# The values' stage of a latent attention: three pairs of banks for the scores, eight places for exponentials, one add in four on VectorE

## The chip, the cores and the metric

The kernel runs on one core of a Trainium2 chip. The metric is the device time of one execution in microseconds; the time of a version is the median of its runs. Everything is computed in float32, apart from some flags of a comparison in bfloat16.

## The reference

Two transformer layers over an input of 2 sequences of 1024 tokens, 512 wide, each with a layer norm ahead of each of its two halves and a residual add behind it. Layer 0 is a gated delta-rule attention and a feed-forward with 4-bit weights. Layer 1 is the attention that the change touches, and a gated feed-forward whose hidden units are kept two of four. Layer 1's attention, for one sequence (16 heads, keys and queries 16 wide, values 32 wide):

```python
q_latent = x @ wq_d                      # 512 -> 64
kv_latent = x @ wkv_d                    # 512 -> 64
q = rope(q_latent @ wq_u)                # 16 heads x 16
k = rope(kv_latent @ wk_u)
v = kv_latent @ wv_u                     # 16 heads x 32
attn = softmax(q @ k.T / sqrt(16))       # no mask: 1024 x 1024 a head
out = (attn @ v) @ wo                    # 512 -> 512
```

Layer 1's feed-forward is `sparsify_2to4(silu(x @ w_gate) * (x @ w_up)) @ w_down` with 2048 hidden units.

## The kernel before

The program is a Python script that is unrolled completely. Four engines (TensorE, VectorE, ScalarE, GpSimd) execute their instructions in exactly the order in which the script issues them. The loads and stores wait in one queue, SP's, and are issued from it one after the other; the planner chooses that order. Waits are derived from the tiles: a tile is taken from a pool with a fixed number of places for its tag (`bufs`), and an instruction that writes a new tile waits until the place that it was given is free.

PSUM has eight banks, which the class `Banks` hands out in three ways. `two` gives a pair of neighbouring banks (1024 columns), two such tiles at a time; `one` gives single banks, two at a time; `acc` holds one bank called `av` and one called `den`, and `side` gives these two in turn to smaller work. So four banks are `two`'s, two are `one`'s and two are `acc`'s.

`weave(main, fill)` sets the order of the work around the change. Both are generators. Each time `main` yields a number, that number is added to what is due, and steps of `fill` are issued until nothing is due. A step of the fill yields `STEP` = 3.4. What is left of the fill at the end of `main` is issued then.

Layer 1's attention of sequence 0 (the generator `first`, `att.run(0, ...)`) is woven with layer 0's feed-forward of sequence 1. In what the text calls the third part, the attention of sequence 1 (the generator `third`, `att.run(1, ...)`) is woven with layer 1's feed-forward of sequence 0 (`Sparse.run`). A step of that fill is four fp32 matmuls of 128x128 by 128x512. In the fourth part layer 1's feed-forward of sequence 1 runs alone (`Sevens`).

`Latent.run` makes the keys and values of a sequence, and then goes through two blocks of 512 queries, each in two stages. `scores` finds each query's largest score, which needs a reduction on VectorE (line 1515), and puts it as a 17th feature beside the 16 of the query, so that it is subtracted by the product itself. `values` is the stage that the change touches. It has 32 units, four groups of four heads by eight tiles of 128 keys. For each unit u:

- `weights(u)` (line 1559): four matmuls, one a head, in four groups of 32 rows of the array, write scores (keys by queries) into two tiles of `banks.two`; ScalarE takes the exponential of each tile (1024 wide, line 1574) into tiles `es`, of which there are six places.
- `gather(u - 1)`: four matmuls add the values' product into the bank `av` (line 1582). After the last unit of a group VectorE copies it to `oT`.
- In the third part (`running` false), for odd u, `pair(u)`: GpSimd adds the four heads' exponentials of unit u into those of unit u - 1, in place, 512 wide (line 1596). Then `total(u - 2)`: four matmuls with ones add the sums of an earlier pair into the bank `den` (line 1603).
- After a group's last total, four `divide` steps are put into the list `late`: VectorE takes the reciprocal of 128 columns of `den` and multiplies `oT` by it (lines 1634, 1635). Up to three of them are issued after each unit.
- The stage yields `per_value` after each unit. It is 3.0 for sequence 0 and 0.1 in the third part.

`project` multiplies `oT` by the output weights `wo`, adds the result to x and stores it. The steps of `output` for the first block are issued between the scores of the second block, and those for the second block at the end; there each of them is followed by a step of fill. In the third part the normalised result is also turned into `xT` for the fourth part (`follow`). With `keep_wo` (the third part) `wo` is loaded once, at the start; without it `output` loads it for each block.

Of the kernel before, what the change touches and what calls it, by code (L numbers as in the profile page):

```python
# [26 lines left out]
F32 = mybir.dt.float32  # L27
# [3 lines left out]
AF = mybir.ActivationFunctionType  # L31
# [5 lines left out]
P = 128  # L37
B, T, DM = 2, 1024, 512
NT = B * T // P
TT = T // P  # L40
KC = DM // P
# [11 lines left out]
NH1, HALF, DV = 16, 16, 32  # L53
LAT = 64
QB = 512
# [1306 lines left out]
class Latent:  # L1362
# [42 lines left out]
            nc.tensor.transpose(ps[:, gr * P : (gr + 1) * P], src[:, 4 * gr : 4 * gr + 4, :], self.core.ident)  # L1405
        nc.scalar.copy(dst, ps.rearrange("p (g t) -> p g t", g=4))

    def run(self, b, side, parked, out, per_score, per_value, keep_wo, running, beside=None, xT=None):

# [2 lines left out]
        core, nc, banks = self.core, self.core.nc, self.banks  # L1414
        p = core.pools(f"l_one{b}", side=side)
        self.tmp = core.pools(f"l_tmp{b}", 1, side=side)
        now = []

        def stage(name):
            if now:  # L1420
                core.pools.close(now.pop())
            if name:
                now.append(f"l_{name}{b}")
                return core.pools(now[0], 2, side=side)

        two = stage("k")
        beside = beside(lambda: two) if beside else iter(())
        for n in self.ns:
            nc.gpsimd.memset(n[:, :, HALF : HALF + 1], 1.0)
        wo = []  # L1430
        if keep_wo:
            wo.append(p.tile([P, KC, DM], F32, name="wo1"))
            nc.sync.dma_start(out=wo[0], in_=self.wo_in)
        lat = p.tile([P, T], F32, name="lat")
        kT = p.tile([P, 4, T], F32, name="kT1")
        v = p.tile([P, TT, NH1, DV], F32, name="v1")
# [116 lines left out]
        def values(q2, oT):  # L1553

            units = [(gr, kt) for gr in range(4) for kt in range(TT)]
            es, av, den, acc = {}, {}, {}, {}
            late = deque()

            def weights(u):
                gr, kt = units[u]  # L1560
                tiles = [banks.two("st_ps") for _ in range(2)]
                for h4 in range(4):
                    r = 32 * h4
                    nc.tensor.matmul(  # L1564
                        tiles[h4 // 2][:, h4 % 2 * 512 : h4 % 2 * 512 + 512],
                        kT[r : r + CR, gr, kt * P : (kt + 1) * P],
                        q2[r : r + CR, gr, :],
                        start=True,
                        stop=True,
                    )  # L1570
                es[u] = []
                for e in range(2):
                    t = two.tile([P, 2, QB], F32, tag="es", bufs=6, name="es")
                    nc.scalar.activation(t.rearrange("p i q -> p (i q)"), tiles[e], AF.Exp, scale=HALF**-0.5)  # L1574
                    es[u].append(t)

            def gather(u):
                gr, kt = units[u]
                if kt == 0:
                    av[gr] = banks.acc.tile([P, QB], F32, tag="av", name="av_ps")  # L1580
                for h4 in range(4):
                    nc.tensor.matmul(  # L1582
                        av[gr][32 * h4 : 32 * h4 + 32, :],
                        v[:, kt, 4 * gr + h4, :],
                        es[u][h4 // 2][:, h4 % 2, :],
                        start=(kt == 0),
                        stop=(kt == TT - 1),
                    )
                if kt == TT - 1:
                    nc.vector.tensor_copy(oT[:, gr, :], av.pop(gr))  # L1590

            def pair(u):

                for h4 in range(4):
                    t = es[u - 1][h4 // 2][:, h4 % 2, :]
                    nc.gpsimd.tensor_add(t, t, es[u][h4 // 2][:, h4 % 2, :])  # L1596

            def total(u):
                gr, kt = units[u]
                if kt == 1:  # L1600
                    den[gr] = banks.acc.tile([P, QB], F32, tag="den", name="den_ps")
                for h4 in range(4):
                    nc.tensor.matmul(  # L1603
                        den[gr][32 * h4 : 32 * h4 + 32, :],
                        self.ones,
                        es[u - 1][h4 // 2][:, h4 % 2, :],
                        start=(kt == 1),
                        stop=(kt == TT - 1),
                    )
                if kt == TT - 1:  # L1610
                    for q in range(QT):
                        late.append(lambda q=q, ps=den[gr]: divide(gr, q * P, ps))

            def add(u):

                gr, kt = units[u]
                if kt == 1:
                    acc[gr] = two.tile([P, 4, QB], F32, tag="acc", bufs=1, name="acc")
                for e in range(2) if kt else ():
                    t = acc[gr][:, 2 * e : 2 * e + 2, :]  # L1620
                    nc.vector.tensor_add(t, es[u - 1][e] if kt == 1 else t, es[u][e])  # L1621

            def total_run(gr):
                den = banks.acc.tile([P, QB], F32, tag="den", name="den_ps")
                for h4 in range(4):
                    nc.tensor.matmul(
                        den[32 * h4 : 32 * h4 + 32, :], self.ones, acc[gr][:, h4, :], start=True, stop=True
                    )
                for q in range(QT):
                    late.append(lambda q=q: divide(gr, q * P, den))  # L1630

            def divide(gr, q, ps):
                rd = two.tile([P, P], F32, tag="rd", name="rd")
                nc.vector.reciprocal(rd, ps[:, q : q + P])  # L1634
                nc.vector.tensor_mul(oT[:, gr, q : q + P], oT[:, gr, q : q + P], rd)

            for u in range(len(units) + 3):
                if u < len(units):
                    weights(u)
                if 0 <= u - 1 < len(units):  # L1640
                    gather(u - 1)
                if running:
                    if 0 <= u - 1 < len(units):
                        add(u - 1)
                    if u > TT and u % TT == 1:
                        total_run(u // TT - 1)
                elif u % 2:
                    if u < len(units):
                        pair(u)
                    if u >= 3:  # L1650
                        total(u - 2)
                yield per_value
                for _ in range(min(3, len(late))):
                    late.popleft()()
            for f in late:
                f()
# [23 lines left out]

        def output(qb, oT):

            if not keep_wo:
                wo[:] = [two.tile([P, KC, DM], F32, tag="wo", bufs=1, name="wo1")]
                nc.sync.dma_start(out=wo[0], in_=self.wo_in)
            turned[0] = fetch(b * TT + qb * QT)
            steps = [lambda: None] + [lambda t=t: project(qb, oT, t) for t in range(QT)]
            if xT is None:
                return steps

            def both(t):
                if t < QT:
                    project(qb, oT, t)
                follow(qb * QT + t)

            return steps[:1] + [lambda t=t: both(t) for t in range(QT + 3)]

        extra = []
        for qb in range(T // QB):
            two = stage("s")  # L1700
# [6 lines left out]
            two = stage("v")  # L1707
            oT = p.tile([P, 4, QB], F32, tag="oT", name="oT1")
            yield from values(q2, oT)
        two = stage("s")  # L1710
# [284 lines left out]
def two_layers(ctx, tc, a):  # L1995
    nc = tc.nc
    core = Core(ctx, tc)
    pools = core.pools
    banks = Banks(ctx, tc)
# [10 lines left out]
    parks = [[tc.dram_tile([P, DM], F32, name=f"park{i}_{n}") for n in range(NT)] for i in range(3)]  # L2010
# [10 lines left out]
    with tc.manual_schedule(engines={ENG.PE, ENG.DVE, ENG.Activation, ENG.Pool}):  # L2021
# [16 lines left out]
        att = Latent(core, banks, pools("l_w", side="right"), a)  # L2038


        def first():
            yield from att.run(0, "right", parks[0], parks[1], 3.4, 3.0, False, True, beside=factors.make)
            xs = pools("x2", side="right")
            core.hold(xs, 0)
            for n in range(TT):
                nc.sync.dma_start(out=core.x[n], in_=parks[1][n])
            yield 2 * STEP
            xT = pools("xT_2", side="right").tile([P, KC, T], F32, name="xT2")
            yield from norms(core, banks, core.x[:TT], xT)
            done.append(xT)  # L2050

        done = []
        factors = Factors(core, a)
# [6 lines left out]
        def third():  # L2060
            xT = pools("xT_3").tile([P, KC, T], F32, name="xT3")
            done.append(xT)
            yield from att.run(1, None, parks[0], parks[1], 3.4, 0.1, True, False, xT=xT)
            x = pools("x3").tile([P, TT, DM], F32, name="x_last")
            held.append(x)
            for n in range(TT, NT):
                core.x[n] = x[:, n - TT, :]
                nc.sync.dma_start(out=core.x[n], in_=parks[1][n])
# [77 lines left out]
```

## Time and profile before

| | |
|---|---|
| median of 3 runs | 3213.23 us (3211.96 to 3216.2) |
| profiled execution | 3214.91 us, span 3213.2 us |
| mean granted TensorE clock | 0.979 |
| busy: TensorE, VectorE, ScalarE, GpSimd | 97%, 60%, 29%, 24% |
| third part's stages of values | 2450 to 2555 us and 2754 to 2863 us |
| last matmul of the fill | 2899 us |
| first matmul of the fourth part | 2906.55 us |

All times inside the profile are microseconds from the start of the span. An instruction is named by its line, its engine and its tiles as "written <- read". A fp32 matmul is recorded as two passes, so that the four matmuls of a unit appear as eight records; neighbouring records of one kind are merged into one row with its start and its length. The row ends with the idle time of the engine before it, and what ended that, in square brackets. A TensorE row is busy while any of its matmuls is in flight, so a busy TensorE need not be one at its best pace. "PEld" is the load of weights into the array.

### The profile page before, as it was taken

To read this page: it belongs to the slowest core of one execution; us is meant where nothing else is said; L and a number is where in the kernel's file an instruction comes from. 1 tells how busy PE (TensorE), PEld (TensorE's weight loads), DVE (VectorE), ACT (ScalarE), POOL (GpSimd) and SP (SyncE) were. 2 spreads that over 40 slices of the span, in tenths; PEclk is the share of its full clock that TensorE was granted. 3 is DMA by queue.
4 is the path that set the end of the run, shared out by engine and by line. 5 is a ranking of instruction groups with operands and counts; after the bars stand their busy time and mean duration, and the time that the engine had idled before them with its cause. 6 is when DMAs were issued, how large, how long until landed. Compare 5 with 4: busy or idle time off the path is not lost.

```text
span 3213.2 us, 35654 instructions
## 1 busy us (share of the span) xinstructions
PE 3106.8 (97%) x13012; PEld 1626.1 (51%) x13012; DVE 1925.1 (60%) x3569; ACT 931.2 (29%) x1338; POOL 766.6 (24%) x822
## 2 busy tenths in 40 slices
PE   7999899999999999999999999999999999999998
PEld 6787754555555554555434444446433243224547
DVE  6888752466666554367577656745674367244766
ACT  5544311122222211311453125522113401432221
POOL 3323101122222211356321221222003600450000
PEclk9999899999999999999999999999999999999999
DMA  2111234132332224246112111142010010015211
GB/s 90 35 29 29 67 96 142 32 122 91 97 95 86 76 94 164 70 137 207 66 37 69 53 48 37 35 141 72 20 40 1 14 53 14 7 37 167 76 46 49
DMA packets 194638, 228.08 MB, mean 71 GB/s; under 512 B 53728, under 2 KB 148448, under 8 KB 194080
## 3 DMA queue, kind: packets, MB, share of 16 engines
q1 hardware_dynamic: 194464, 225.81, 22.2%
q8 instruction: 103, 1.69, 0.2%
q14 instruction: 71, 0.58, 0.1%
HBM read 153.11 MB, written 72.61 MB: 70 GB/s over the span
## 4 chain that ended last, share of the span: by engine, by line
PE 81%; DVE 9%; POOL 2%; issue 2%; ACT 2%; DMA 2%; SPq 1%; DVEq 0%; POOLq 0%; ACTq 0%
PE z_ps L1018 23%; PE o_ps L201 12%; PE z_ps L1064 8%; PE u_ps L201 5%; PE g_ps L201 5%; PE st_ps L1564 5%; PE s_ps L1506 4%; PE av_ps L1582 3%; PE proj_ps L201 2%; PE small_ps L630 1%; PE wide_ps L640 1%; DVE cv L469 1%; PE wide_ps L558 1%; DVE rd L1634 1%; PE den_ps L1603 1%
## 5 line engine op out<-in xcount | busy, mean ns | idle before, releaser
L991 ACT COPY part<-z_ps 128x512 f32<-128x512 f32 x288 | 168.7, 586 | 738.4 <-PE z_ps L1018 505.5
L1018 PE MATMUL z_ps<-xT,z_left 128*128 128x512 f32 x768 | 361.8, 601 | 3.1 <-DMA z_left<-in_w_gate 3.0
L1515 DVE TENSOR_REDUCE top<-s_ps 128x2 f32<-128x1024 f32 x256 | 301.0, 1217 | 80.4 <-PE s_ps L1506 80.3
L1574 ACT ACTIVATE es<-st_ps 128x1024 f32<-128x1024 f32 x256 | 248.3, 1021 | 175.9 <-PE st_ps L1564 171.0
L1018 PE MATMUL z_ps<-xt,z_left 128*128 128x512 f32 x576 | 274.3, 598 | 1.2 <-DVE z_h L1036 1.0
L1018 PEld LDWEIGHTS z_ps<-xT,z_left 128*128 128x128 f32 x768 | 142.0, 191 | 191.6 <-issue 164.0
L201 PE MATMUL o_ps<-w_down,h 128*128 128x512 f32 x512 | 229.6, 599 | 0.4 <-DVE part L1052 0.4
L1596 POOL TENSOR_TENSOR es<-es 128x512 f32<-128x512 f32 x128 | 159.3, 1276 | 148.7 <-ACT es L1574 78.0
L1018 PE MATMUL z_ps<-xT,w_left 128*128 128x512 f32 x384 | 181.5, 602 | 5.0 <-DVE part L1052 2.7
L1564 PE MATMUL st_ps<-q,kT 17*128 17x512 f32 x1024 | 178.3, 650 | 4.3 <-ACT es L1574 1.1
L1018 PEld LDWEIGHTS z_ps<-xt,z_left 128*128 128x128 f32 x576 | 106.2, 190 | 145.7 <-issue 123.3
L1052 DVE TENSOR_TENSOR part<-z_ps,part 128x512 f32<-128x512 f32 x108 | 74.4, 689 | 174.1 <-PE z_ps L1018 168.5
L1506 PE MATMUL s_ps<-kT,q 16*128 16x512 f32 x1024 | 156.6, 647 | 6.6 <-DVE top L1515 6.6
L201 PEld LDWEIGHTS o_ps<-w_down,h 128*128 128x128 f32 x512 | 95.2, 191 | 110.5 <-issue 106.3
L201 PE MATMUL proj_ps<-xT,wqkv 128*128 128x256 f32 x576 | 136.6, 392 | 12.2 <-ACT gw L427 12.2
L1582 PE MATMUL av_ps<-es,v 128*32 128x512 f32 x1024 | 138.9, 615 | 0.0
L1018 PE MATMUL z_ps<-xt,w_left 128*128 128x512 f32 x288 | 137.0, 598 | 0.7 <-DVE part L1052 0.7
L1053 POOL TENSOR_TENSOR h<-h,part 128x512 f32<-128x512 f32 x48 | 66.5, 1387 | 280.1 <-DVE part L1052 280.1
L1621 DVE TENSOR_TENSOR acc<-acc,es 128x1024 f32<-128x1024 f32 x96 | 131.7, 1419 | 0.0
L201 PEld LDWEIGHTS proj_ps<-xT,wqkv 128*128 128x128 f32 x576 | 109.3, 195 | 31.6 <-ACT gw L427 15.1
L1036 DVE TENSOR_TENSOR h<-z_ps,part 128x512 f32<-128x512 f32 x84 | 57.9, 690 | 102.4 <-PE z_ps L1018 89.3
L201 PE MATMUL o_ps<-sdown,h 128*128 128x512 f32 x256 | 117.1, 601 | 0.0
(311 smaller groups left out, 5164.9 us busy)
## 6 DMA issues: line engine op xcount, KB each, us to landing
sums<-factor SPq DMA_DIRECT2D x24, 512.0 KB, 3.3
kept_gate<-w_left SPq DMA_DIRECT2D x12, 896.0 KB, 3.7
kept_up<-w_left SPq DMA_DIRECT2D x12, 896.0 KB, 3.9
z_left<-kept_gate SPq DMA_DIRECT2D x12, 896.0 KB, 4.6
z_left<-kept_up SPq DMA_DIRECT2D x12, 896.0 KB, 4.6
kept_down<-w_down SPq DMA_DIRECT2D x16, 512.0 KB, 3.0
wd<-kept_down SPq DMA_DIRECT2D x16, 512.0 KB, 4.2
xl<-park SPq DMA_DIRECT2D x32, 256.0 KB, 2.7
```

Of the source, the lines that this page charges most:

```text
L201: nc.tensor.matmul(ps, lhsT, rhs, start=(i == 0), stop=(i == len(pairs) - 1))
L991: self.core.nc.scalar.copy(t, src)
L1018: self.core.nc.tensor.matmul(ps, left[l][:, k, :], self.right[r][:, k, :], start=(first and k == 0), stop=(k == 1), skip_group_check=True,)
L1052: nc.vector.tensor_add(v, ps, v)
L1064: nc.tensor.matmul(ps[:, i * dm : (i + 1) * dm], left[l][:, k, i * P : (i + 1) * P], right[r][k], start=(first and i == 0 and k == 0), sto ...
L1506: nc.tensor.matmul(tiles[h4 // 2][:, h4 % 2 * 512 : h4 % 2 * 512 + 512], q1s[t][r : r + HALF, gr, :], kT[r : r + HALF, gr, j * 512 : (j + ...
L1515: nc.vector.tensor_reduce(top[:, j, h : h + 2], tiles[e].rearrange("p (i k) -> p i k", i=2), AX.X, ALU.max, negate=True)
L1564: nc.tensor.matmul(tiles[h4 // 2][:, h4 % 2 * 512 : h4 % 2 * 512 + 512], kT[r : r + CR, gr, kt * P : (kt + 1) * P], q2[r : r + CR, gr, :], ...
L1574: nc.scalar.activation(t.rearrange("p i q -> p (i q)"), tiles[e], AF.Exp, scale=HALF**-0.5)
L1582: nc.tensor.matmul(av[gr][32 * h4 : 32 * h4 + 32, :], v[:, kt, 4 * gr + h4, :], es[u][h4 // 2][:, h4 % 2, :], start=(kt == 0), stop=(kt == ...
L1596: nc.gpsimd.tensor_add(t, t, es[u][h4 // 2][:, h4 % 2, :])
L1621: nc.vector.tensor_add(t, es[u - 1][e] if kt == 1 else t, es[u][e])
```

## The change

In the third part (`alone`, that is `per_value == 0`):

- the two tiles of scores of a unit come from `spot`, which gives a tile of `banks.two` twice and then two tiles of `banks.one`, in turn; a tile made of single banks gets two exponentials of 512 columns instead of one of 1024;
- `es` has eight places instead of six;
- the fourth of a pair's adds is issued on VectorE, the other three stay on GpSimd;
- after a group's last total, VectorE copies the bank `den` whole to a tile `dn` in SBUF, and the divisions read that, with the reciprocal in place;
- `per_value` is 0 instead of 0.1, so that no step of the fill is issued within the stage;
- `keep_wo` is gone: the output weights are loaded by `output`, for each of the two blocks.

For sequence 0 the stage keeps its two pairs, its six places and its order; there `es` is summed by `add`, which is not touched.

```diff
+        alone = per_value == 0
...
-        if keep_wo:
-            wo.append(p.tile([P, KC, DM], F32, name="wo1"))
-            nc.sync.dma_start(out=wo[0], in_=self.wo_in)
...
-                tiles = [banks.two("st_ps") for _ in range(2)]
+                tiles = [spot() for _ in range(2)]
...
-                        tiles[h4 // 2][:, h4 % 2 * 512 : h4 % 2 * 512 + 512],
+                        tiles[h4 // 2][h4 % 2],
...
-                for e in range(2):
-                    t = two.tile([P, 2, QB], F32, tag="es", bufs=6, name="es")
-                    nc.scalar.activation(t.rearrange("p i q -> p (i q)"), tiles[e], AF.Exp, scale=HALF**-0.5)
+                for tile in tiles:
+                    t = two.tile([P, 2, QB], F32, tag="es", bufs=8 if alone else 6, name="es")
+                    if len(tile) == 3:
+                        nc.scalar.activation(t.rearrange("p i q -> p (i q)"), tile[2], AF.Exp, scale=HALF**-0.5)
+                    else:
+                        for i in range(2):
+                            nc.scalar.activation(t[:, i, :], tile[i], AF.Exp, scale=HALF**-0.5)
                     es[u].append(t)
+
+            def spot():
+                count[0] += 1
+                if alone and count[0] % 3 == 0:
+                    return [banks.one("st_ps") for _ in range(2)]
+                tile = banks.two("st_ps")
+                return [tile[:, :QB], tile[:, QB:], tile]
...
-                    nc.gpsimd.tensor_add(t, t, es[u][h4 // 2][:, h4 % 2, :])
+                    eng = nc.vector if alone and h4 == 3 else nc.gpsimd
+                    eng.tensor_add(t, t, es[u][h4 // 2][:, h4 % 2, :])
...
                 if kt == TT - 1:
+                    dn = two.tile([P, QB], F32, tag="dn", bufs=1, name="dn")
+                    nc.vector.tensor_copy(dn, den.pop(gr))
                     for q in range(QT):
-                        late.append(lambda q=q, ps=den[gr]: divide(gr, q * P, ps))
+                        late.append(lambda q=q: divide(gr, q * P, dn, dn[:, q * P : (q + 1) * P]))
...
-            def divide(gr, q, ps):
-                rd = two.tile([P, P], F32, tag="rd", name="rd")
+            def divide(gr, q, ps, rd=None):
+                if rd is None:
+                    rd = two.tile([P, P], F32, tag="rd", name="rd")
                 nc.vector.reciprocal(rd, ps[:, q : q + P])
...
-            if not keep_wo:
-                wo[:] = [two.tile([P, KC, DM], F32, tag="wo", bufs=1, name="wo1")]
-                nc.sync.dma_start(out=wo[0], in_=self.wo_in)
+            wo[:] = [two.tile([P, KC, DM], F32, tag="wo", bufs=1, name="wo1")]
+            nc.sync.dma_start(out=wo[0], in_=self.wo_in)
...
-            yield from att.run(1, None, parks[0], parks[1], 3.4, 0.1, True, False, xT=xT)
+            yield from att.run(1, None, parks[0], parks[1], 3.4, 0, False, xT=xT)
```

## The prediction

> **What bounds the kernel now.** I read the views in this order: the page's groups, to find the lines that the change touches; the third part's busy time by stretches; the order of time, engine by engine, inside one stretch; and the granted clock around its ends.
>
> The two groups of the page that the change touches (columns: operation, count, busy us, mean ns of one, then idle time before and what ended it):
>
> ```profile
> L1574 ACT ACTIVATE es<-st_ps 128x1024 f32<-128x1024 f32 x256 | 248.3, 1021 | 175.9 <-PE st_ps L1564 171.0
> L1596 POOL TENSOR_TENSOR es<-es 128x512 f32<-128x512 f32 x128 | 159.3, 1276 | 148.7 <-ACT es L1574 78.0
> ```
>
> Only the third part uses POOL's adds (128 of them: two stages of values, sixteen pairs of units each, four heads). So that is where to look. In order of time, TensorE over one pair of units (start, length):
>
> ```profile
> 2459.10 1.07 PE L1582 MATMUL av_ps<-es,v 128*32 128x512 f32 x8
> 2460.10 1.32 PE L1564 MATMUL st_ps<-q,kT 17*128 17x512 f32 x8
> ...
> 2467.43 1.06 PE L1582 MATMUL av_ps<-es,v 128*32 128x512 f32 x8
> 2468.31 1.04 PE L1603 MATMUL den_ps<-es,ones 128*32 128x512 f32 x8
> 2469.28 1.14 PE L1564 MATMUL st_ps<-q,kT 17*128 17x512 f32 x8
> 2470.36 1.06 PE L1582 MATMUL av_ps<-es,v 128*32 128x512 f32 x8
> 2471.53 2.04 PE L1564 MATMUL st_ps<-q,kT 17*128 17x512 f32 x8
> 2473.51 1.06 PE L1582 MATMUL av_ps<-es,v 128*32 128x512 f32 x8
> 2474.39 1.04 PE L1603 MATMUL den_ps<-es,ones 128*32 128x512 f32 x8
> ...
> 2486.98 1.07 PE L1603 MATMUL den_ps<-es,ones 128*32 128x512 f32 x8 [0.26 <-DVE rd L1634]
> ```
>
> ScalarE and GpSimd over the same pair:
>
> ```profile
> 2470.46 1.94 ACT L1574 ACTIVATE es<-st_ps 128x1024 f32<-128x1024 f32 x2 [1.81 <-PE st_ps L1564]
> 2472.79 1.94 ACT L1574 ACTIVATE es<-st_ps 128x1024 f32<-128x1024 f32 x2 [0.39 <-PE st_ps L1564]
> ```
>
> ```profile
> 2468.62 4.95 POOL L1596 TENSOR_TENSOR es<-es 128x512 f32<-128x512 f32 x4 [1.13 <-PE av_ps L1582]
> 2474.70 4.96 POOL L1596 TENSOR_TENSOR es<-es 128x512 f32<-128x512 f32 x4 [1.13 <-PE av_ps L1582]
> ```
>
> A pair takes 6.08 us (2468.31 to 2474.39), and one chain fills it. Scores of the even unit start at 2469.28; their exponentials start 1.18 later; two of these take 1.94; only then is the second pair of banks free for the second half of the odd unit's scores. That is why the odd unit's scores take 2.04 and the even unit's 1.14: the four heads normally stream side by side, and here two run, then two more, 0.98 each. Behind them come the values' product (0.88 to the next start) and the denominator (0.97), and the next even unit. 1.18 + 1.94 + 0.15 + 0.98 + 0.88 + 0.97 = 6.10. So two pairs of banks pace the stage. GpSimd is idle 1.13 of each 6.08, ScalarE 2.2, and TensorE's 97% hides a split, not work. Once in a group of eight units the denominator also waits for its bank, which four reciprocals still read: 24.79 us a group (GpSimd's 2493.39 to 2518.18) against 4 x 6.08 = 24.32.
>
> The ends of the two stages, by stretches (busy us of PE, PEld, DVE, ACT, POOL; then the granted clock):
>
> ```profile
> 2562.71:2566.12 3.41, 0.71 (x2) 0.00 (x0) 3.31 (x7) 0.00 (x0) 0.00 (x0) 1.00 0.00 0
> 2566.12:2576.36 10.24, 9.03 (x15) 3.53 (x16) 6.98 (x12) 0.00 (x0) 0.00 (x0) 0.50 0.01 2
> 2753.86:2757.27 3.41, 2.30 (x14) 0.61 (x12) 2.54 (x6) 1.62 (x2) 0.00 (x0) 1.00 0.20 77
> 2757.27:2770.92 13.65, 13.65 (x56) 2.75 (x52) 0.00 (x0) 6.24 (x7) 6.18 (x6) 0.50 0.01 1
> 2772.00:2857.00 85.00, 82.60 (x552) 20.26 (x552) 21.54 (x27) 54.32 (x57) 67.51 (x56) 1.00 0.00 1
> ```
>
> TensorE went to half clock twice: behind the first stage, and at the second's start, which has no fill between its first two units and so leaves TensorE idle for 1.11 us there.
>
> **The change, part by part.**
>
> *Three pairs of banks.* Tiles of scores go round three pairs (the third made of two single banks), so a tile waits for the exponential of the tile three back. For an odd unit that is, for its first half, the second tile of the unit before the last (read long since), and, for its second, the first tile of the even unit. The chain loses one exponential: 1.18 + 1.02 + 0.15 + 0.98 + 0.88 + 0.97 = 5.18. The floor with no wait is 1.08 + 1.00 + 1.08 + 0.88 + 0.97 = 5.01 (starts in the lines above). I take 5.2 a pair. A tile in single banks takes two 512-wide exponentials; the nearest row, a 512-wide ScalarE copy, is 0.586 us, so 1.17 instead of 1.02. ScalarE then needs, for four tiles of which 4/3 are such, 4 x 1.02 + 1.33 x 0.15 = 4.28: under 5.2.
>
> *One add in four on VectorE.* GpSimd's chain falls from 4.95 to 3 x 1.24 = 3.71. VectorE's add is 0.69 (its 512-wide add from a bank; half of its 1.22 for 1024 from SBUF gives 0.61). If the two disturb each other: next to GpSimd the 128-wide product of the division took up to 1.41 against 0.29 alone, so up to 1.12 longer, and GpSimd's four adds took 5.06 instead of 4.95. Ends: 3.71 and 3.71 + 0.69 = 4.40, both under 5.2. Cover: the total is due two units later, some 5.2 + 1.95 after the scores began, and the adds are through at 2.2 + 4.4 = 6.6. Without this edit GpSimd's 4.95 plus its shortest restart (2462.55 - 2457.16 = 5.39) would pace the stage. VectorE's queue behind the add holds the divisions; it has four adds, two copies of 0.69 and 5.0 us of divisions in a group of 20.8.
>
> *Eight places for exponentials.* Four units in flight instead of three: nothing by itself, needed by the step above (an exponential of unit u+3 would otherwise wait for adds of unit u).
>
> *Sums copied out.* A copy of about 0.69 on VectorE frees the denominator's bank before the four divisions (4 x 1.24) instead of after; the 0.47 a group goes, three times a stage. The copy itself lies beside TensorE's next two units.
>
> *No fill in the stages.* With 0 instead of 0.1 per step, the fill steps at 2451.25, 2555.02 and 2858.46 (eight matmuls, 3.43 us each at full pace) run later, when TensorE has nothing else: I count them as work in both kernels, at no gain. Bounds for where they land: the last turn before the fourth part has TensorE waits of 0.89, 1.66 and 3.02, so up to 2.6 less, or nothing.
>
> *A stage, walked.* Scores 0 at 0; scores 1 start at 1.08 and their second half at 1.18 + 1.02 + 0.15 = 2.35, done at 3.33; the first values' product follows, scores 2 start at 4.4. Fifteen pairs at 5.2 bring 82.4. Then a product of 1.0 and the wait for GpSimd's last adds: last scores at 79.3, adds from 81.6, three of 1.24 plus 0.55 for the disturbance, last matmuls 0.55: end at 86.4. Before: first stage 2450.18 to 2555.02 = 104.84, less 3.43 of fill, 101.4; second 2754.48 to 2863.09 = 108.61, less 3.43, 105.2 (it has the half clock). Gains 15.0 and 18.8.
>
> *Behind the first stage.* The next scores wait for a reduction that stands in VectorE's queue behind the four divisions, and those stood behind the fill's add and comparisons. Before: 2555.02 to 2567.33, two fill steps in it, so 12.31 - 7.26 = 5.05 of loss. After: copy 0.9, divisions 5.0, first reduction 1.2, so 7.1 with one fill step of 3.6: 3.5. Gain 1.5. TensorE still idles 2.4 us there, so I leave the half clock (about 3.9 us of loss) as it is.
>
> *The output weights, loaded twice.* The 1 MB load leaves p, and with it its 8 KB per partition, and is issued at each output(), on SP ahead of the loads of x (SP already stood there 111.8 us for the end of the stage, so what is behind it starts no earlier). It takes 5.8 (4.3 to 7.4) from issue to landing. Behind the first stage the first projection comes some 9 us in: hidden. At the end, the projection waited until 2869.45, 6.36 after the last sum, for reciprocals that held its bank; with the copy that wait is gone, and the load, landing at 0.3 + 5.8 = 6.1, takes its place: 0; ends -2.7 (its place is free early) and +1.4.
>
> Sum: 15.0 + 18.8 + 1.5 + 0 = 35.3. The profiled execution took 3214.9 (span 3213.2); 3179.6 by it. The median of the runs is 1.7 lower: **3178**.
>
> *A rule against the trace.* The half clock came after stretches of 3.41 us in which TensorE was busy 0.71 and 2.30 us, and stayed until one was full. The Trainium skill, "TensorE: Matmul & The Clock Gate", Part 1, has TensorE fall to half rate after at least one idle window of about 3.4 us; by that neither stretch should have fallen, the trace differs, and the measurement decides. By the page alone no stretch of the new walk falls, and the sum would be 3.9 larger, 3174.
>
> **The rivals.**
>
> *Half clock at the starts.* Both stages now start with bare scores, where the first used to have fill. For it: the second stage lost 6.4 there (14.86 to its first total against 12.06 - 3.6). Against: the idle 1.11 shrinks to about 0.3. Price: 6.4 each, 3191 with both.
>
> *GpSimd and VectorE hold each other up*, and the adds pace the stage at 5.4 (its shortest restart now) instead of 5.2: 30 pairs x 0.2 = 6, so 3184; at 5.6, 3190. For it: the 1.41 above. Against: GpSimd lost 0.1 in 4.95. The Trainium skill, "SBUF — State Buffer", has a VectorE instruction with two SBUF inputs contend with a GpSimd one that reads SBUF; the 1.41 agrees.
>
> *The change does not do what it says*: the places are handed out so that an odd unit's exponentials take those that its own total, two units back, must free. Then total 0.97, exponential 1.02, adds 3.71 and hand-overs run in a ring of about 6.1, and the stage stays: 3213 less 1.5. Against: today's odd units start exponentials before that total.
>
> *Slower: the half clock stays.* At half clock a pair takes 2.02 + 1.87 + 2.23 + 1.71 + 1.77 = 9.6 (2761.51 to 2771.11), 4.4 over 5.2. From eight pairs (35.3 / 4.4) on the gain is gone; one whole stage costs 70: 3248. For it: at 2757 TensorE needed 13.65 to get out. Against: 85 us at 1.00 with worse splits than the new ones.
>
> **How the numbers follow.** Forecast 0.60, half clock at the starts 0.14, adders 0.11, no effect 0.05, slower 0.10. The runs of before spread 0.13%, so 0.2% (6.4 us) is about what can be told from none. The first three are faster: 0.85; same 0.05; slower 0.10. Low end: 3178 less 3.9 (no half clock behind the first stage), 2.7 (the load), 2.6 (the last turn) and 30 x 0.19 (the floor of 5.01) = 3163; I take 3165. High end: 3191 plus the adders' 6, and 1.4 for the load, 3199; I take 3200.
>
> **What would show it.** Right: a group of eight units takes 20.8 instead of 24.79; odd units' scores take near 1.3, not 2.04; GpSimd's busy time falls by a quarter; no reciprocal before a denominator; the last projection waits for a load. Wrong: a period still at 6.1, or scores at twice their length over whole stages.

## The result and the profile after

The changed kernel takes 3183.57 us (median of 4 runs, 3179.73 to 3185.09) against 3214.1 us before; the ratio is 0.991, with a 95% interval of 0.9897 to 0.9924. The profiled execution took 3184.22 us, span 3182.5. That is faster by some 30 us, where 3178 was forecast, inside the range of 3165 to 3200. That the total came out near is in part luck: the two stages brought little over half of what they were to bring, and stretches that were put at next to nothing made up for it.

What was predicted of the steady state is there. TensorE in order of time in the first stage, one pair of units and its neighbours (start, length):

```profile
2496.16 1.04 PE L1615 MATMUL den_ps<-es,ones 128*32 128x512 f32 x8
2497.13 1.14 PE L1562 MATMUL st_ps<-q,kT 17*128 17x512 f32 x8
2498.20 1.06 PE L1593 MATMUL av_ps<-es,v 128*32 128x512 f32 x8
2499.20 1.41 PE L1562 MATMUL st_ps<-q,kT 17*128 17x512 f32 x8
2500.53 1.06 PE L1593 MATMUL av_ps<-es,v 128*32 128x512 f32 x8
2501.42 1.04 PE L1615 MATMUL den_ps<-es,ones 128*32 128x512 f32 x8
```

A pair takes 5.26 us (2496.16 to 2501.42) instead of 6.08; the odd unit's scores take 1.41 instead of 2.04, and no row shows a wait for a reciprocal. GpSimd over the same stretch:

```profile
2496.49 4.19 POOL L1608 TENSOR_TENSOR es<-es 128x512 f32<-128x512 f32 x3 [1.06 <-PE av_ps L1593]
```

Three adds take 3.96 to 4.19, not three quarters of 4.95 (3.71): VectorE's add beside them costs GpSimd up to four tenths of the 1.24 that it takes off it. GpSimd still waits 1.0 to 1.3 for TensorE in each pair, so this costs the pace nothing.

What was not in the sum of the forecast is at the two starts. TensorE, ScalarE and VectorE together at the start of the second stage:

```profile
2734.98 2.04 PE L1562 MATMUL st_ps<-q,kT 17*128 17x512 f32 x12
...
2736.19 1.28 ACT L1573 ACT_TABLE_LOAD   x1 [3.94 <-PE st_ps L1562]
2737.49 1.94 ACT L1573 ACTIVATE es<-st_ps 128x1024 f32<-128x1024 f32 x2
2738.56 2.08 PE L1562 MATMUL st_ps<-q,kT 17*128 17x512 f32 x4 [1.54 <-ACT es L1573]
...
2740.57 1.94 PE L1593 MATMUL av_ps<-es,v 128*32 128x512 f32 x8
```

The load of ScalarE's table of exponentials stands behind the wait for the first scores and delays the exponentials by 1.28. From 2737.87 on TensorE runs at half clock. The stretches of both starts and of the rest of both stages (us, busy us of PE, PEld, DVE, ACT, POOL, then the granted clock):

```profile
2451.16:2454.57 3.41, 3.20 (x17) 1.09 (x16) 0.69 (x1) 1.88 (x3) 0.00 (x0) 1.00 0.00 0
2454.57:2464.81 10.24, 10.24 (x46) 2.03 (x48) 1.71 (x1) 5.87 (x9) 4.17 (x3) 0.50 0.01 2
2465.00:2538.00 73.00, 73.00 (x560) 20.47 (x556) 38.36 (x44) 54.31 (x74) 57.81 (x42) 1.00 0.00 1
2734.46:2737.87 3.41, 2.56 (x14) 0.79 (x12) 0.69 (x1) 1.67 (x2) 0.00 (x0) 1.00 0.00 0
2737.87:2751.53 13.66, 12.97 (x52) 2.53 (x52) 2.76 (x2) 7.50 (x10) 5.30 (x4) 0.50 0.00 1
2752.00:2824.00 72.00, 72.00 (x552) 20.23 (x552) 36.59 (x44) 54.17 (x74) 56.29 (x41) 1.00 0.00 1
```

Both stages lose the full clock, the first for 10.24 us although TensorE was busy 3.20 of the 3.41 us before it fell.

And the end of the third part has no gap any more. TensorE there:

```profile
2872.70 3.60 PE L201 MATMUL o_ps<-sdown,h 128*128 128x512 f32 x8
2876.14 3.60 PE L1018 MATMUL z_ps<-xT,z_left 128*128 128x512 f32 x8
```

Before, the last fill step began at 2895.69 and the fourth part at 2906.55; now the one follows the other.

Laid side by side, in us, with a fill step counted at 3.43 us wherever it runs:

| stretch | before | after | gain, fill apart | predicted |
|---|---|---|---|---|
| up to the first stage's scores | 2450.18 | 2451.52 | -1.3 | 0 |
| first stage | 104.84 (1 fill step) | 92.20 | 9.2 | 15.0 |
| from it to the second stage | 199.46 (1 more step) | 191.26 | 4.8 | 1.5 |
| second stage | 108.61 (1 step) | 94.87 | 10.3 | 18.8 |
| to the fourth part | 43.46 (5 steps) | 46.29 (8 steps) | 7.5 | 0 |
| fourth part | 306.65 | 306.36 | 0.3 | 0 |
| sum | | | 30.8 | 35.3 |

### The profile page after: what moved, and what is told of

Its sections match the earlier page's. It is cut to its first block, busy times and chain, and to the rows that moved or that the text cites. A ratio compares the mean times of both kernels' runs of the same rounds, so it can differ in the third digit from the quotient of the medians.

```text
span 3182.5 us, 35790 instructions
## 1 busy us (share of the span) xinstructions
PE 3080.6 (97%) x13012; PEld 1624.7 (51%) x13012; DVE 1962.9 (62%) x3609; ACT 933.1 (29%) x1380; POOL 739.5 (23%) x790
## 4 chain that ended last, share of the span: by engine, by line
PE 76%; DVE 5%; POOL 2%; issue 2%; DMA 1%; ACT 1%; SPq 0%; DVEq 0%; POOLq 0%; ACTq 0%
PE z_ps L1018 24%; PE o_ps L201 12%; PE z_ps L1064 8%; PE u_ps L201 5%; PE g_ps L201 5%; PE st_ps L1562 5%; PE av_ps L1593 4%; PE s_ps L1504 4%; PE den_ps L1615 1%; PE wide_ps L640 1%; PE small_ps L630 1%; PE hT_ps L1405 1%; PE small_ps L201 1%; PE wide_ps L397 1%; PE wide_ps L558 1%
## 5 line engine op out<-in xcount | busy, mean ns | idle before, releaser
L1573 ACT ACTIVATE es<-st_ps 128x1024 f32<-128x1024 f32 x214 | 209.9, 1022 | 129.5 <-PE st_ps L1562 124.4
L1608 POOL TENSOR_TENSOR es<-es 128x512 f32<-128x512 f32 x96 | 132.5, 1408 | 148.5 <-PE av_ps L1593 144.9
L1562 PE MATMUL st_ps<-q,kT 17*128 17x512 f32 x1024 | 162.0, 657 | 1.7 <-ACT es L1573 1.7
L1161 DVE TENSOR_TENSOR x<-x,o_ps 128x512 f32<-128x512 f32 x64 | 43.9, 686 | 122.3 <-PE o_ps L201 122.2
```

What stands on the lines that cost most here:

```text
L1562: nc.tensor.matmul(tiles[h4 // 2][h4 % 2], kT[r : r + CR, gr, kt * P : (kt + 1) * P], q2[r : r + CR, gr, :], start=True, stop=True,)
L1573: nc.scalar.activation(t.rearrange("p i q -> p (i q)"), tile[2], AF.Exp, scale=HALF**-0.5)
L1608: eng.tensor_add(t, t, es[u][h4 // 2][:, h4 % 2, :])
```

## The experiments

Theory, after the result: two pairs of banks paced the stage, and with three the walk of the prediction holds (86.4 us a stage) as long as TensorE keeps its clock; the clock falls at the starts because these hold almost nothing but scores, which use 17 of each 32 rows of the array. Rivals: GpSimd's adds were the pace; the clock falls by chance alone, or by idle time alone; the other edits pay for themselves, or not at all. The loads of the output weights were not undone by themselves.

### One edit undone at a time

**Two pairs.** The scores' tiles come from `banks.two` alone.

```diff
-                if alone and count[0] % 3 == 0:
+                if False and count[0] % 3 == 0:
```

> Only the third pair of banks is undone. Theory (the banks pace the stage): a pair of units takes 6.08 us again instead of 5.25, odd units' scores take 2.04 instead of 1.40, so each stage is about 15 x 0.83 = 12.5 us longer and the kernel about 25 us slower than the changed one, near 3208. Rival (GpSimd's adds paced the stage before, and the fourth add on VectorE is what freed it): the pair stays below 5.5 us and the kernel within 8 us of 3184.

Measured 3212.72 in one run (before 3206.96 on that chip). TensorE, with the split scores back:

```profile
2493.58 1.04 PE L1615 MATMUL den_ps<-es,ones 128*32 128x512 f32 x8
2494.55 1.14 PE L1562 MATMUL st_ps<-q,kT 17*128 17x512 f32 x8
2495.62 1.06 PE L1593 MATMUL av_ps<-es,v 128*32 128x512 f32 x8
2496.89 2.04 PE L1562 MATMUL st_ps<-q,kT 17*128 17x512 f32 x8 [0.20 <-ACT es L1573]
2498.86 1.06 PE L1593 MATMUL av_ps<-es,v 128*32 128x512 f32 x8
```

6.16 us a pair, in every pair at full clock, although GpSimd had only three adds and there were eight places for exponentials. The stages take 107.4 and 112.0, 15 and 17 us more. Of these 0.91 in each of fifteen pairs, 13.7, is the pace; the rest goes with longer stretches of half clock at the starts, 13.65 and 23.89 us instead of 10.24 and 13.65. The banks were the pace; GpSimd was not. In this one run every other edit together, without the third pair, wins nothing.

**Four adds on GpSimd.**

```diff
-                    eng = nc.vector if alone and h4 == 3 else nc.gpsimd
+                    eng = nc.gpsimd
```

> Only the add on VectorE is undone: GpSimd adds all four heads. Theory: GpSimd's 4.95 us plus its shortest restart of 0.44 paces the stage at about 5.4 us a pair instead of 5.25, so 15 x 0.15 x 2 = 4.5 us, and the wait for the last adds is 0.8 longer in each stage: about 3190. Rival (banks alone pace it): 5.25 a pair and 3185. Rival (GpSimd was the pace all along): 6.08 a pair and about 3208.

Measured 3179.58 in one run. GpSimd:

```profile
2464.41 4.97 POOL L1608 TENSOR_TENSOR es<-es 128x512 f32<-128x512 f32 x4 [0.75 <-PE av_ps L1593]
2469.65 4.96 POOL L1608 TENSOR_TENSOR es<-es 128x512 f32<-128x512 f32 x4 [0.28 <-PE av_ps L1593]
2475.02 5.02 POOL L1608 TENSOR_TENSOR es<-es 128x512 f32<-128x512 f32 x4 [0.40 <-PE av_ps L1593]
```

Pairs take 5.24 to 5.42, 5.33 on average, about as expected, and GpSimd is now idle 0.23 to 0.45 in a pair once the stage runs steadily. So the add on VectorE is worth 0.08 a pair, little over 1 us a stage. The run's time, under the expected 3190, is no argument against it: its first stage kept the full clock (90.4 us), which the changed kernel's had not.

**Six places.**

```diff
-                    t = two.tile([P, 2, QB], F32, tag="es", bufs=8 if alone else 6, name="es")
+                    t = two.tile([P, 2, QB], F32, tag="es", bufs=6, name="es")
```

> Only the places for exponentials go back from eight to six. Theory of the prediction (needed, since an exponential would wait for adds of three units before): the pair lengthens, by at most the adds' 4.18 us against the 5.25 in which they are hidden now; I expect 5.4 to 5.7 a pair and 3188 to 3197. Rival: six are enough with places handed out as they come free; 5.25 a pair and 3184.

Measured 3165.89, and the expectation missed: it is faster. Both stages take 86.80 us with the full clock throughout, 0.4 from the walk of the prediction, and a pair takes 5.16 to 5.20. TensorE in a pair:

```profile
2480.80 1.04 PE L1615 MATMUL den_ps<-es,ones 128*32 128x512 f32 x8
2481.78 1.14 PE L1562 MATMUL st_ps<-q,kT 17*128 17x512 f32 x8
2482.85 1.06 PE L1593 MATMUL av_ps<-es,v 128*32 128x512 f32 x8
2483.84 1.31 PE L1562 MATMUL st_ps<-q,kT 17*128 17x512 f32 x8
2485.08 1.07 PE L1593 MATMUL av_ps<-es,v 128*32 128x512 f32 x8
2485.97 1.04 PE L1615 MATMUL den_ps<-es,ones 128*32 128x512 f32 x8
```

The even unit's exponentials start 1.17 and 1.15 after its scores here (2482.95 and 2488.09), with eight places 1.21 and 1.25 (2498.34 and 2503.64); and ScalarE loads its table ahead of the second stage's scores, at 2721.5. In every run with eight places and bare starts that load stood behind the scores. That the places bring another wait ahead of the exponentials fits both; which wait it is was not separated.

**The sums not copied.**

```diff
-                    dn = two.tile([P, QB], F32, tag="dn", bufs=1, name="dn")
-                    nc.vector.tensor_copy(dn, den.pop(gr))
...
-                        late.append(lambda q=q: divide(gr, q * P, dn, dn[:, q * P : (q + 1) * P]))
+                        late.append(lambda q=q, ps=den[gr]: divide(gr, q * P, ps))
```

> Only the copy of the sums is undone: the divisions read the bank. Theory: the denominator waits for the fourth reciprocal once in a group, at least 0.47 us as before the change, three times in each of two stages, and the last projection waits for the reciprocals instead of the 1 MB load: 3 to 6 us, about 3187. Rival: the copy itself costs VectorE 0.7 us that delays its add, so that nothing or a gain of 1 to 2 us is left: 3182 to 3184.

Measured 3237.65: 54 us over the changed kernel, and slower than before by 31. The expectation missed widely. TensorE where one group of units ends and the next begins:

```profile
2487.27 1.06 PE L1593 MATMUL av_ps<-es,v 128*32 128x512 f32 x8
2490.91 1.64 PE L1615 MATMUL den_ps<-es,ones 128*32 128x512 f32 x8 [2.58 <-DVE rd L1647]
2492.48 2.09 PE L1562 MATMUL st_ps<-q,kT 17*128 17x512 f32 x8
```

The wait for the fourth reciprocal left TensorE idle for 0.26 to 0.3 and lengthened a group by 0.47 at the old pace; at the new one it is 2.58, 15.5 in the six waits: a faster stage reaches the bank sooner, and VectorE's divisions now stand behind an add in its queue (the first reciprocal starts 1.04 after the total's end at 2483.93, before the change 0.14). Behind each of the six waits the clock fell, for 10 to 20 us at a time, and at both starts; the expectation of no_copy_rows32 below counts one wait too few. One of the smallest terms of the prediction is the one that the change can least do without.

### What the clock follows

**The same kernel again.** Six places, timed over three rounds; the program is that of six_places.

> The changed kernel with six places for exponentials instead of eight, timed against the kernel before in three rounds. In the look, its stages took 86.8 us each, with no half clock at their starts and 5.17 us a pair, against 92.3 and 94.9 of the changed kernel. Theory A (eight places cost something by themselves: exponentials start 0.07 us later each pair, and the table load falls behind the wait for the second stage's first scores): a ratio to before of 0.986 to 0.988, clearly under the changed kernel's 0.991. Theory B (the half clock fell or not by where its windows of 3.41 us happened to lie): over several executions the ratio comes back to 0.990 or 0.991, and the granted clock differs between executions.

3176.36, ratio 0.9886 (0.9868 to 0.9904). The interval overlaps the changed kernel's, so this time alone does not tell six places from eight. In the execution profiled here the first stage fell to half clock, 10.24 us, and took 91.2; in the one profiled above it did not, and took 86.8. The stretch of 3.41 us ahead of the fall with what follows, and then the stretch of the other execution that holds most of its start, with what follows:

```profile
2446.95:2450.36 3.41, 3.20 (x17) 1.09 (x16) 0.69 (x1) 1.89 (x3) 0.00 (x0) 1.00 0.00 0
2450.36:2460.60 10.24, 10.24 (x46) 2.03 (x48) 1.72 (x1) 5.85 (x9) 4.18 (x4) 0.50 0.01 2
```

```profile
2446.79:2450.21 3.42, 3.21 (x24) 0.85 (x16) 0.25 (x1) 2.86 (x5) 0.00 (x0) 1.00 0.00 0
2450.21:2453.62 3.41, 3.41 (x28) 0.95 (x24) 1.27 (x1) 2.94 (x5) 2.96 (x3) 1.00 0.00 0
```

TensorE was busy 3.20 and 3.21 us. What differs is which matmuls these were: in the stretch that fell nearly all 17 records are scores, in the other eight of the 24 are the values' product. Within a profile the clock's changes lie whole multiples of 3.413 us apart, and where that grid lies differs from execution to execution. Over the starts of the runs here with 17-row scores, three pairs, no fill and no table load in the way, the clock fell at all three where a point of the grid lay 3.06 to 3.13 us after the first scores, and at none of the four where it lay at 0.6, 2.5 or 2.6. So it is chance, but chance in the place of the grid, and at these starts it takes a stretch of hardly anything but scores. The Trainium skill, "TensorE: Matmul & The Clock Gate", Part 1, describes free-running windows of that length, which agrees; it has the clock fall after an idle window, and here it fell after one that was 94% busy.

**A fill step at the start.**

```diff
-                yield per_value
+                yield 3.4 if alone and u == 0 else per_value
```

> The changed kernel with one step of fill (four full matmuls) behind the first unit's scores in both stages. Theory A (what throws TensorE to half clock at the starts is that the first 3.5 us hold bare scores, which use 17 of each 32 rows, and one short wait): no half clock at either start, 4.5 us won in the first stage and 7.2 in the second, ratio near 0.987. Theory B (chance alone, a third of all starts): ratio 0.990 to 0.991. If the fill is missed at the end, where it hides the loads of the fourth part, up to 5 us are given back.

3175.16, ratio 0.988 (0.9863 to 0.9898). Both stages take 91.17 with 3.43 of fill in them, 87.7 without it, at the full clock. In the second a point of the grid lay 3.08 after the first scores, where bare scores had fallen in three of three, and here TensorE was busy for the whole stretch. At the end, from the second stage to the fourth part, there are now six steps of fill in 41.0: 20.4 besides the fill, against 18.9 in the changed kernel (46.29 - 8 x 3.43), so 1.5 is given back, not 5.

**Scores over 32 rows.** Keys and queries lie in groups of 32 rows, of which 15 hold zeros; the matmul takes them all.

```diff
-                        kT[r : r + CR, gr, kt * P : (kt + 1) * P],
-                        q2[r : r + CR, gr, :],
+                        kT[r : r + (32 if alone else CR), gr, kt * P : (kt + 1) * P],
+                        q2[r : r + (32 if alone else CR), gr, :],
```

> The changed kernel with scores over 32 rows a head instead of 17 in the third part; the added rows hold zeros, so the result is the same. Theory A (the clock is granted by how much of the array works, and rows count): TensorE's starts keep the full clock, ratio near 0.987. Theory B (only the time in which matmuls run counts, or zeros don't count): as the changed kernel, 0.991. The pace of a pair stays 5.25 either way.

3179.19, ratio 0.9898 (0.9878 to 0.9919). In the profile neither start fell. The second is a fair comparison with that of four_gpsimd: both have the table load and its 1.54 of idle, and the grid lies within 0.1 us of the same place behind the first scores. The stretch that decides, in four_gpsimd (17 rows, with what follows) and here (32 rows, with what follows):

```profile
2733.23:2736.64 3.41, 2.21 (x16) 0.61 (x20) 0.00 (x0) 3.40 (x6) 0.00 (x0) 1.00 0.00 0
2736.64:2746.88 10.24, 10.24 (x46) 2.09 (x48) 0.00 (x0) 4.49 (x6) 7.49 (x7) 0.50 0.01 2
```

```profile
2736.65:2740.06 3.41, 2.16 (x16) 0.57 (x17) 0.00 (x0) 3.40 (x6) 0.00 (x0) 1.00 0.00 0
2740.06:2743.47 3.41, 3.41 (x28) 1.05 (x32) 1.27 (x1) 2.88 (x5) 3.33 (x3) 1.00 0.00 0
```

Equally busy, and only the 17-row one falls. One pair of starts is thin, and the median alone does not tell rows32 from the changed kernel, so the next run asks where there are six chances.

**Scores over 32 rows, the sums not copied.**

> The sums are not copied, as in no_copy, where TensorE waited 2.6 us for the fourth reciprocal at six group borders and lost the full clock at all of them but one; and the scores run over 32 rows a head (zeros in the added rows). Theory A (rows of the array count for the clock): the waits stay at 2.6 us each, 15.5 in all, but the clock falls at two of the borders or fewer, each stage is near 100 us instead of 118 and the kernel near 3200. Theory B (only the wait counts, or zeros do not): stages near 118 us and 3238 as in no_copy.

3190.91, against 3237.65 with 17 rows. What TensorE waited for is the same in both, down to the digit; this line is word for word in both answers:

```profile
PE den_ps L1615 <- DVE rd L1647: 15.5, 6, 2.6
```

The stages by stretch, with 17 rows and then with 32:

```profile
2454.00:2572.60 118.60, 109.87 (x645) 25.94 (x644) 44.52 (x45) 64.15 (x86) 65.91 (x48) 0.78 0.00 1
2764.80:2882.80 118.00, 107.95 (x642) 25.97 (x641) 44.02 (x45) 65.53 (x87) 65.89 (x48) 0.80 0.00 1
```

```profile
2450.50:2546.70 96.20, 87.46 (x645) 23.77 (x644) 41.13 (x45) 64.14 (x86) 65.98 (x48) 1.00 0.00 1
2738.70:2837.60 98.90, 88.84 (x642) 24.06 (x641) 41.23 (x45) 65.43 (x87) 65.95 (x48) 0.98 0.00 1
```

The clock falls once, for 3.41 us, instead of behind six waits and at both starts. These are not six equal chances: the grid cuts the waits of the two runs in different places, and the three waits of a stage much alike. In the stretches of 3.41 us that decide, TensorE was busy 0.83 to 0.95 us in four of the six with 17 rows, less than in any with 32 (1.28, which fell, and 1.67 to 1.93). The emptiest four prove nothing for the rows; the fullest of 17 rows does, beside two of 32 (17 rows first):

```profile
2856.50:2859.91 3.41, 1.95 (x16) 0.28 (x12) 3.34 (x4) 2.67 (x4) 2.40 (x3) 1.00 0.00 0
2859.91:2873.56 13.65, 12.54 (x56) 2.58 (x56) 4.72 (x5) 4.00 (x6) 5.17 (x4) 0.50 0.01 1
```

```profile
2478.52:2481.94 3.42, 1.93 (x16) 0.26 (x9) 3.35 (x5) 2.68 (x4) 2.40 (x3) 1.00 0.00 0
2795.96:2799.37 3.41, 1.67 (x16) 0.50 (x16) 3.38 (x4) 0.00 (x0) 3.13 (x3) 1.00 0.00 0
2799.38:2802.79 3.41, 3.41 (x32) 1.01 (x28) 0.26 (x1) 2.84 (x4) 0.00 (x0) 1.00 0.00 0
```

The same holds over all stretches of the grid at full clock between 2440 and 2900 us of the thirteen profiles, 1646 of them. By busy time those behind which the clock fell (34) and those behind which it held are mixed: 0.20 to 0.94 of the stretch, and 0.49 to 1.00. If the time in which TensorE has only scores is counted by their rows, at 16/32 or 17/32 (in full where they have 32), they come apart but for a narrow band: at most 0.56 where it fell, at least 0.49 where it held. So rows at work count for the clock, also where they multiply zeros, and neither busy nor idle time alone decides. Of the 54 us that the missing copy cost, some 15 are the waits, and most of the rest is the clock: with 32 rows the two stages are 18 us longer than in rows32, with 17 rows 49 us longer than in the changed kernel.

### Where the fill runs, and what is best

**The kernel before without fill in its stages** (0 instead of 0.1 due after each unit, nothing else).

> The kernel before with 0 instead of 0.1 due after each unit of the third part's values, nothing else. Theory (three fill steps moved to the end cost nothing there, since they cover the loads of the fourth part's first weights): end of the second stage to the first matmul of the fourth part about 46 us with eight fill steps, as in the changed kernel, instead of 43.4 with five: 7 us won at the end. Against it stands the first stage's start, which has no cover any more and loses up to 6.4 if the clock falls, and the wait for GpSimd's last adds in the second, 3.4. In sum 3204 to 3213, if before is 3213. Rival (moved fill is paid in full, 3.4 us a step): the end takes 53 us, and the kernel is 3213 to 3220.

3222.61 in one run, over both expected spans; on that chip the kernel before ran from 3200.1 to 3221.5, so the total says little. By stretches: the end took 45.9 with eight fill steps (before 43.46 with five), 7.8 won, as in the changed kernel. Both stages lost the clock at their starts for 13.65 us each and took 108.66 and 108.60. Free of fill that is 7.2 and 3.4 more than before. So without the third pair the moved fill wins 7.8 at the end and loses 10.6 in the stages, 7.2 of it in the first, whose start had kept the clock before.

**Six places with a fill step, and six places with 32 rows.**

> Six places and one step of fill behind the first unit's scores of both stages. If both effects are real and apart: stages near 90 us with 3.4 us of fill in them, no half clock at the starts, ratio 0.985 to 0.987. If six places alone already keep the clock: as six_again, or up to 5 us slower, since the two fill steps are missing at the end.

3171.24, ratio 0.9871 (0.9854 to 0.9889): both stages 90.1 with 3.43 of fill, no half clock in them. This interval lies under the changed kernel's (0.9897 to 0.9924), so this version beats both the kernel before and the changed one.

> Six places for exponentials and scores over 32 rows, no fill in the stages. If rows count for the clock, both stages take 86.8 us in each execution, and all eight fill steps stay at the end: ratio 0.985 to 0.987, at or under six_fill's 0.987. If they do not count, the first stage falls to half clock in some executions as in six_again: 0.988.

3169.14 (3166.71 to 3177.88), ratio 0.9882 (0.9859 to 0.9905), both stages 86.80 in the profile. Not told apart from six_fill, and the ratio is nearer the rival's 0.988 than the expected 0.985 to 0.987, so the times do not decide; one of its starts does. In the profile a point of the grid lay 3.38 us after the first scores of the first stage, and the stretch ahead of it is scores over 32 rows but for its ends:

```profile
2447.71:2451.13 3.42, 3.21 (x21) 1.16 (x24) 0.69 (x1) 2.21 (x3) 0.00 (x0) 1.00 0.00 0
```

TensorE was busy 3.21 us, as in the stretches of 17 rows that fell at 3.20, and the clock held.

## Why the prediction was right, and where not

- **The pace** was right: the chain through one exponential, 5.2 predicted, 5.25 with eight places, 5.17 with six; two_pairs shows that it is the banks.
- **The walk of a stage** (86.4) was right where the clock held (86.8 with six places, 87.7 with eight), and 5.8 and 8.5 short in the changed kernel. The step that failed is that the bare starts would cost no clock: the sum has no term for it. The rival of the half clock at the starts (chance 0.14) is what happened, at 4.5 and 7.2 where 6.4 each was its price: first scores to the fifth unit's took 14.1 and 16.8, by the walk 9.6. Its argument against (idle shrinks to 0.3) failed: the idle did shrink, to 0.21 in the first stage, and the clock does not go by idle time: it fell with TensorE busy 3.20 of 3.41 us. In the second the table load, which the sum did not have, added 1.28, so that the idle there grew to 1.54.
- **Eight places** were called needed; they cost some 0.08 a pair. The assumption behind it, that an exponential would wait for the adds of three units before, does not hold at this pace.
- **The add on VectorE** was bounded by 3.71 and 4.40 for GpSimd, measured 3.96 to 4.19; without it 5.33 a pair, predicted 5.4. GpSimd's adds take 132.5 us in all instead of 159.3, a sixth less, where a quarter was named as a sign.
- **The copy** was costed at the old wait, 0.47 a group; undone in the new kernel the wait is 2.58 and the clock goes with it. Here the step that failed priced a wait at the pace of before.
- **Behind the first stage** 1.5 was predicted and 4.8 came: the idle there went from 3.91 to 2.13, and the half clock, which had been left as it was, shrank from 10.24 to 3.41. In the other runs it lasted 3.41 or 6.83 there, so part of this gain is the place of the grid.
- **The end** was put at 0, with at most 2.6 to win at the last turn and 2.7 at the load, and brought 7.5. TensorE's waits there sum to 2.80 instead of 8.23, and the 3.41 us of half clock behind the wait for the reciprocals, from 2869.94 on, some 1.7 of loss that the prediction had not seen, are gone. The loads for the fourth part had started at 2901.91, behind the last fill step, and now start at 2870.23, ahead of the last one. before_no_fill, where only the fill is moved, wins 7.8 there. The output weights landed as thought: TensorE waited 1.40 for them, from the stage's end 5.10 to the projection instead of 6.36.
- The 9.2 + 10.3 of the stages fell short by 14.3; the end and the middle gave 10.8 more. That is why the total was near, and it was luck.

## What to carry to other kernels

Where four small matmuls run side by side, look for the wait that splits them: here two and two cost 0.98 twice instead of 1.07 once, and the engine shows as busy all the while. Price an edit that frees a buffer at the new pace, by undoing it in the changed kernel, not by the wait that the old one shows. And where a stretch consists of matmuls over few rows, give them zeros up to the full group of rows, or put full matmuls between. Here the zeros cost nothing, 5.25 a pair with 17 rows and with 32, and the clock held at all six starts that were profiled with them.

## What the runs showed of the hardware that was not expected

The clock fell after a stretch of 3.41 us with TensorE 3.20 us busy, when nearly all of it was scores over 17 rows in each group of 32, and held with 3.21 us busy when a third of the records were matmuls over all 128 rows. With zeros in the other 15 rows it held after 3.21 us busy with hardly anything but scores, and of six waits of 2.58 us it fell behind one, for 3.41 us, where with 17 rows it had fallen behind all six. Beside GpSimd's adds, VectorE's 512-wide add took 0.76 to 1.76 us, 1.16 in the middle, instead of the 0.69 of its add from a bank, and three adds of GpSimd up to 4.19 instead of 3.71.
